# Gaps of 64 and 192 bytes between SBUF tiles, so that the operands of a transformer block's MLP lie at other remainders of 256 bytes

## The chip, the core and the metric

The kernel runs on one core of one Trainium2 chip. A time is the device time of one execution in microseconds; the median of several runs is given. One execution is also recorded by the hardware profiler, and all rows of the profile are from that one.

## The reference

One block of a diffusion transformer (PixArt style) on 16 images of 256 tokens with 256 channels, 16 heads of 16 channels, all in fp32: self-attention, cross-attention to 256 context tokens, and an MLP. Cut to what is computed:

```python
shift_a, scale_a, gate_a, shift_m, scale_m, gate_m = split(silu(c) @ W_mod + b_mod, 6)
q, k, v = heads(modulate(ln(x), shift_a, scale_a) @ W_qkv + b_qkv)
x = x + gate_a * (softmax(q @ k.T * scale) @ v @ W_proj + b_proj)
q = heads(ln(x) @ W_qc + b_qc);  k, v = heads(ln(context) @ W_kvc + b_kvc)
x = x + softmax(q @ k.T * scale) @ v @ W_cproj + b_cproj
h = gelu(modulate(ln(x), shift_m, scale_m) @ W_mlp1 + b_mlp1)      # 256 -> 1024
x = x + gate_m * (h @ W_mlp2 + b_mlp2)                             # 1024 -> 256
```

## The kernel before

**Precision.** Products of activations and weights are made of three: each operand is split into a rounded part and a rest (`...h` and `...l`, tiles of type fp32r), and `mm3` (line 411) and `mm3_tok` (line 420) add up high by high, high by low, low by high. A call of `PE.matmul` takes its stationary operand first in the source's `a` and its moving operand in `b`: 128 stationary columns, 256 moving elements.

**Attention, from the start to about 550 us.** 32 units, 16 of self- and 16 of cross-attention, are worked off in turn, each in 8 beats (`beat`, line 1041). A beat issues scores of the next unit (`s_tile`, line 661, into PSUM tile `s`, for the row maxima), transposed scores of the present one (`t_part`, line 707, into `st`, for the exponential), and beside them projections of later units (`lanes`, line 448) and the products with v (`av_part`, line 737, into `o`). Unit n keeps q and k in the SBUF tile `big[n % 3]`, so both operands of its scores are in one tile. `to_stack` (line 459) makes q and k: its `high` writes `h_...` (tag `qkh`), its `low` `l_...` (tag `qkl`), and DMAs on SP's queue carry both into `big`. `one_rows` (line 939) puts rows of ones from the tile `ones` into `big` by DMA.

**The MLP, the last 180 us.** Images go in the order 0, 2 to 15, 1; each has 4 chunks c of 256 hidden channels. For a chunk,

- `mlp_first` (line 829) multiplies with `W1`: 2 x 6 matmuls into `ph`, stationary `W1` (in `wself`), moving the transposed input `xTh_m`, `xTl_m` (tags `xTh`, `xTl`);
- `mlp_gelu` (line 860) makes `hf` (tag `pt`), `hh` (tag `qkh`) and `hl` (tag `qkl`) on ACT and POOL;
- `mlp_second` (line 877) multiplies with `W2`: 2 x 6 matmuls into `s` or `st` by turns of images, stationary `hh` and `hl`, moving `W2`, which is in `big[2]`. With the last chunk DVE makes the output (`mt`, `y`) from the gate `gm` and `xg` (`xmg` in the profile), and SP's queue stores it.

The chunks of image 1 are prepared ahead (`mlp_ahead`, line 848), and their `hh` and `hl` lie in `big[0]`. The loop at line 1239 issues for its chunk i: the gelu of i + 1, at each image's chunk 0 the transposition `mlp_T` of the next image (`psT_m`), `mlp_first` of i + 2, `mlp_second` of i - 1. Without a transposition between them, `ph` and `s`/`st` pieces of 12 matmuls alternate on TensorE. In the last four chunks there is no `mlp_first` left. `mlp_residual` (line 794) loads `gm` on SP's queue, behind the store of the image before.

**Where tiles lie.** SBUF tiles are placed one after the other in the order of their first declaration, `const` tiles (lines 78 to 143) ahead of `work` tiles, whose tags come in the order of first use with `bufs` buffers each; a size is rounded up to 32 bytes in each partition. With the sizes in bytes of a partition, the remainder of the start by 256 is:

| tiles | bytes each | start | remainder |
|---|---|---|---|
| `ident` | 512 | 17024 | 128 |
| `big0`, `big1`, `big2` | 16384 | 17568 and on | 160 |
| `v0` to `v2`, `wself`, `ones` | 4096, 16384, 1024 | 66720 and on | 160 |
| `brow`, weights of cross-attention `wqc` to `wcp` | 512, 2048 | 96416 and on | 160 |
| small tiles, `cb` (1024) at 115008 | | 113312 and on | |
| tag `qkh` (first use `c_sb`) | 3 x 2048 | 117088 | 96 |
| tag `pt` | 5 x 4096 | 123232 | 96 |
| tags `x`, `g`, `x1`, `c`, `xn` | 2048 | 143712 and on | 96 |
| tags `xTh`, `xTl` | 4 x 2048 each | 181088 | 96 |
| tag `qkl` | 3 x 2048 | 197472 | 96 |
| tag `mx`, then the rest | | 203616 and on | 96, then 224 |

The last tile ends 32 bytes below 229376. Rows, k blocks and column blocks of 128 elements inside the tiles above are multiples of 512 bytes, so an operand of an MLP matmul has its tile's remainder.

**Order.** TensorE, ACT, DVE, POOL and SP issue in program order (`InOrder`, line 40), which is written out by hand in the tables of `E_` (line 55).

Of the kernel before, what the change touches and what calls it, by code (L numbers as in the profile page):

```python
# [10 lines left out]
F32 = mybir.dt.float32  # L11
F32R = mybir.dt.float32r
# [4 lines left out]
P = 128  # L17
# [4 lines left out]
def pixart_block(  # L22
# [8 lines left out]
    B, N, H = x.shape  # L31
# [28 lines left out]
    const = ctx.enter_context(tc.tile_pool(name="const", bufs=1))  # L60
    work = ctx.enter_context(tc.tile_pool(name="work", bufs=2))
# [6 lines left out]
    def ps_gen(name, tag=None):  # L68


        if tag is None and ps_turn[0] is not None:
            ps_turn[0] ^= 1
            tag = (SHORT, LONG)[ps_turn[0]]
        tag = tag or SHORT
        return psum.tile([P, 512], F32, tag=tag, name=name, bufs=2)
# [6 lines left out]
    mhalf = const.tile([P, 2], F32, name="mhalf")  # L82
    POOL.memset(mhalf, -0.5)

    big = [const.tile([P, 2, 8, N], F32R, name=f"big{i}") for i in range(3)]
    vts = [const.tile([P, NT, NH, 32], F32, name=f"v{i}") for i in range(3)]
    wself = const.tile([P, 16, H], F32R, name="wself")
    ones = const.tile([8, N], F32, name="ones")
    DVE.memset(ones, 1.0)


    BMOD, BQKV, BQC, BKVC, BM1 = 0, 12, 18, 20, 24
    ct_ = work.tile([B, 2, H], F32, tag="qkh", name="c_sb", bufs=3)
    c_sb, th = ct_[:, 0], ct_[:, 1]
    SP.dma_start(c_sb, cond)
    X = {}
# [43 lines left out]
    bT = const.tile([P, 32], F32, name="bT")  # L140
    bP = const.tile([P, 2, 2, KC], F32, name="bP")
    sT = const.tile([P, KC, B], F32, name="sT")
    cb = const.tile([P, H], F32, name="cb")
    gd = dram.tile([B, 4, H], F32, name="gd", bufs=1)
    cd = dram.tile([1, H], F32, name="cd", bufs=1)

# [264 lines left out]
    def mm3(dst, W, f, xT):  # L411

        n = 0
        for k in range(KC):
            for a, b in ((W[0], xT[0]), (W[0], xT[1]), (W[1], xT[0])):
                PE.matmul(dst, a[:, k, f * P:(f + 1) * P], b[:, k],
                          start=(n == 0), stop=(n == 3 * KC - 1))
                n += 1
# [40 lines left out]
    def to_stack(W, src, bias, dst, which, name):  # L459

        o = Box()
        lo_row = (2, 1)[which]

        o.W, o.src, o.tok, o.name = W, src, False, name

        def first():
            o.ps = ps_gen(f"ps_{name}", LONG)
            mm3(o.ps[:, 0:N], W, 0, src.xT)  # L470

        def third():
            mm3(o.ps[:, N:], W, 1, src.xT)

        def second():
            third()
            high()

        def high():
            o.hi = work.tile([P, KC, N], F32R, tag="qkh", name=f"h_{name}", bufs=3)  # L480
            for f in range(KC):
                ACT.activation(o.hi[:, f], o.ps[:, f * N:(f + 1) * N], AF.Identity, bias=bias[f])

        def low():
            o.lo = work.tile([P, KC, N], F32R, tag="qkl", name=f"l_{name}", bufs=3)
            for f in range(KC):
                DVE.scalar_tensor_tensor(o.lo[:, f], o.ps[:, f * N:(f + 1) * N], bias[f], o.hi[:, f],
                                         ALU.add, ALU.subtract)

        def low_pool():  # L490
            o.lo = work.tile([P, KC, N], F32R, tag="qkl", name=f"l_{name}", bufs=3)
            y = work.tile([P, KC, N], F32, tag="y", name=f"y_{name}", bufs=1)
            for f in range(KC):
                ACT.activation(y[:, f], o.ps[:, f * N:(f + 1) * N], AF.Identity, bias=bias[f])
            POOL.tensor_tensor(o.lo, y, o.hi, ALU.subtract)

        def send(part, q=SP):

            row = (0, 3 - lo_row, lo_row)[part]
            q.dma_start(dst[row:row + 4 * 31 + 1:4].bitcast(F32), (o.hi if part < 2 else o.lo).bitcast(F32))  # L500

        o.send = send
        o.parts = [first, second, low]
        o.third = third
        o.low_pool = low_pool
        o.high, o.low = high, low
        o.send_high = lambda: [send(part) for part in range(2)]
        o.send_low = lambda: send(2)
        o.steps = [first, second]
        return o  # L510
# [799 lines left out]
```

## Time and profile before

| | us |
|---|---|
| median of 3 runs | 733.66 |
| lowest and highest | 732.69, 734.03 |
| the profiled execution | 732.58 |
| its span, first to last instruction | 730.8 |

The busy time of an engine is the union of its instructions. "PE" rows are matmuls, "PEld" rows loads of a stationary operand. A matmul row's own duration (0.28 us) is longer than the distance to the next one, since matmuls overlap; so distances between starts, or the length of a piece of the chain divided by its matmuls, tell the pace. A piece of the chain of waits in order of time has its start, its length in us, what ran, and the number of instructions merged in it (x12). In rows of the time line stand the start, the length, engine, line, operation, out<-in, shapes and count. All instructions have line 51, a helper's, so pieces are told apart by their tiles.

### The profile page before, as it was taken

The page shows a single profiled execution, that of the slowest core. Times are in us where ns is not written, and L with a number is a line of the kernel's source. Part 1 is how long each engine was busy: PE and PEld are TensorE (multiplying, and loading weights), DVE is VectorE, ACT ScalarE, POOL GpSimd, SP SyncE. Part 2 cuts the span into 40 slices and gives each one's busy share as a digit, 9 for nine tenths or more (in the row PEclk, how much of TensorE's full clock was granted, in tenths as well). Part 3 has the DMA queues.
Part 4 walks back from the last instruction along what each step waited for, and adds up shares of the span by engine and source line. Part 5 has one row for each costly group of instructions (what it writes and reads, how often), then busy time and mean ns, then how long its engine had stood idle before and what let it go on. Part 6 is the DMA issues. An engine that isn't in the chain of part 4 may idle for free.

```text
span 730.8 us, 22489 instructions
## 1 busy us (share of the span) xinstructions
PE 720.2 (99%) x9007; PEld 598.9 (82%) x9007; DVE 557.8 (76%) x876; ACT 557.7 (76%) x971; POOL 542.0 (74%) x533
## 2 busy tenths in 40 slices
PE   9999999999999999999999999999999999999997
PEld 8777777777777777777777778787679999999997
DVE  4878888888888788888888887878665677777743
ACT  5577888888888888888888888887867677666661
POOL 8455788887876868786686899988867988656551
PEclk9999999999999999999999999999999999999999
DMA  8365445544545555454655646456223231312212
GB/s 261 136 227 162 159 157 183 173 161 164 184 135 178 178 183 175 164 174 136 197 167 173 212 170 190 147 199 191 87 75 110 60 88 57 87 45 88 60 43 73
DMA packets 81387, 106.14 MB, mean 145 GB/s; under 512 B 16450, under 2 KB 44388, under 8 KB 81284
## 3 DMA queue, kind: packets, MB, share of 16 engines
q1 hardware_dynamic: 80180, 103.92, 44.1%
q8 instruction: 71, 1.16, 0.7%
q10 hardware_dynamic: 1104, 0.79, 0.3%
q14 instruction: 32, 0.26, 0.1%
HBM read 35.89 MB, written 8.98 MB: 61 GB/s over the span
## 4 chain that ended last, share of the span: by engine, by line
PE 93%; DVE 2%; DMA 1%; ACT 1%; POOL 1%; issue 1%; SPq 0%; ACTq 0%; POOLq 0%
PE s L51 18%; PE o L51 16%; PE st L51 14%; PE ph L51 12%; PE ps_P_s L51 4%; PE ps_k L51 4%; PE ps_qc L51 3%; PE ps_q L51 3%; PE ps_v_c L51 3%; PE ps_P_c L51 2%; PE ps_kc L51 2%; PE ps_v_s L51 2%; PE psT_c L51 2%; PE psT_s L51 1%; DVE mx L51 1%; PE psT_q L51 1%
## 5 line engine op out<-in xcount | busy, mean ns | idle before, releaser
L51 DVE TENSOR_REDUCE mx<-s 128x4 f32<-128x1024 f32 x252 | 308.1, 1222 | 88.5 <-PE s L51 85.1
L51 ACT ACTIVATE pt<-st 128x1024 f32<-128x1024 f32 x256 | 263.1, 1028 | 53.4 <-PE st L51 53.2
L51 PE MATMUL o<-pt,v 128*32 128x256 f32 x2048 | 137.0, 385 | 0.0
L51 PE MATMUL s<-big 63*128 63x256 f32 x1008 | 118.4, 307 | 1.7 <-DVE mx L51 0.7
L51 PE MATMUL st<-big 64*128 64x256 f32 (+1 forms) x1040 | 108.9, 283 | 1.6 <-DMA big<-l_q 0.8
L51 PE MATMUL ph<-xTh_m,wself 128*128 128x256 f32 x512 | 101.4, 283 | 0.0
L51 POOL TENSOR_TENSOR hl<-hf,hh 128x512 fp32r<-128x512 f32 x60 | 81.2, 1370 | 21.5 <-ACT hh L51 21.4
L51 PEld LDWEIGHTS s<-big 63*128 63x128 f32 x1008 | 78.2, 185 | 21.2 <-issue 9.3
L51 PEld LDWEIGHTS st<-big 64*128 64x128 f32 (+1 forms) x1040 | 81.9, 186 | 4.8 <-ACT pt L51 2.1
L51 PEld LDWEIGHTS o<-pt,v 128*32 128x32 f32 x2048 | 53.4, 109 | 38.9
L51 PEld LDWEIGHTS ph<-xTh_m,wself 128*128 128x128 f32 x512 | 82.7, 189 | 1.2 <-issue 0.4
L51 PE MATMUL ph<-xTl_m,wself 128*128 128x256 f32 x256 | 71.5, 279 | 0.0
L51 ACT ACTIVATE hf<-ph,bT 128x256 f32<-128x256 f32 x112 | 47.0, 473 | 21.7 <-PE ph L51 21.1
L51 ACT ACTIVATE hh<-ph,bT 128x256 fp32r<-128x256 f32 x112 | 47.2, 476 | 21.1 <-PE st L51 8.9
L51 PEld LDWEIGHTS ph<-xTl_m,wself 128*128 128x128 f32 x256 | 48.2, 188 | 0.0
L51 PE MATMUL s<-big,hh 128*128 128x256 f32 x256 | 46.0, 278 | 0.0
L51 DVE TENSOR_SCALAR xn_m<-x,mv_m,rs_m 128x256 f32<-128x256 f32 x28 | 33.6, 1239 | 14.8 <-POOL rs_m L51 14.8
L51 POOL TENSOR_SCALAR xn_c<-c,mv_c,rs_c 128x256 f32<-128x256 f32 x32 | 39.0, 1229 | 1.7
L51 PE MATMUL st<-big,hh 128*128 128x256 f32 x224 | 40.2, 278 | 0.0
L51 POOL TENSOR_SCALAR xn_q<-x,mv_q,rs_q 128x256 f32<-128x256 f32 x31 | 37.8, 1230 | 1.7
L51 PEld LDWEIGHTS s<-big,hh 128*128 128x128 f32 x256 | 39.0, 188 | 0.0
L51 ACT COPY oT<-o 128x512 f32<-128x512 f32 x64 | 37.6, 587 | 1.4 <-PE o L51 1.4
(226 smaller groups left out, 2120.9 us busy)
## 6 DMA issues: line engine op xcount, KB each, us to landing
big<-h_kc SPq DMA_DIRECT2D x32, 256.0 KB
big<-h_qc SPq DMA_DIRECT2D x32, 256.0 KB
big<-h_k SPq DMA_DIRECT2D x31, 256.0 KB
big<-h_q SPq DMA_DIRECT2D x31, 256.0 KB
big<-l_k SPq DMA_DIRECT2D x16, 256.0 KB
big<-l_q SPq DMA_DIRECT2D x16, 256.0 KB
g<-gd SPq DMA_DIRECT2D x16, 256.0 KB
U_s<-oT SPq DMA_DIRECT2D x32, 128.0 KB
```

Source lines behind the costliest of these rows:

```text
L51: i = f(*a, **k)
```

## The change

A helper `gap` declares a tile that nothing reads or writes. Six gaps are put between tiles: 192 bytes ahead of `big2` and 64 behind it, 64 ahead of the tag `qkh` and 192 behind it, 64 ahead of the tag `qkl` and 192 behind it. So `big2` (with `W2`) starts at remainder 96, and `hh` and `hl` at 160; all tiles behind each pair of gaps have the remainder that they had. To make room, `ones` no longer has a tile of its own: it is the first 8 partitions of `cb`, which is declared in its place and gets its own values later (`mlp_w1`, line 898, by a DMA on SP's queue).

```diff
-    big = [const.tile([P, 2, 8, N], F32R, name=f"big{i}") for i in range(3)]
+    def gap(pool, n, name):
+
+        pool.tile([P, n // 4], F32, tag=name, name=name, bufs=1)
+
+    big = []
+    for i in range(3):
+        if i == 2:
+            gap(const, 192, "gap_w2")
+        big.append(const.tile([P, 2, 8, N], F32R, name=f"big{i}"))
+    gap(const, 64, "gap_v")
     vts = [const.tile([P, NT, NH, 32], F32, name=f"v{i}") for i in range(3)]
     wself = const.tile([P, 16, H], F32R, name="wself")
-    ones = const.tile([8, N], F32, name="ones")
+    cb = const.tile([P, H], F32, name="cb")
+    ones = cb[:8]
     DVE.memset(ones, 1.0)
...
+    gap(work, 64, "gap_h")
     ct_ = work.tile([B, 2, H], F32, tag="qkh", name="c_sb", bufs=3)
+    gap(work, 192, "gap_pt")
...
-    cb = const.tile([P, H], F32, name="cb")
...
         def low():
+            if name == "k0":
+                gap(work, 64, "gap_l")
             o.lo = work.tile([P, KC, N], F32R, tag="qkl", name=f"l_{name}", bufs=3)
+            if name == "k0":
+                gap(work, 192, "gap_mx")
```

## The prediction, on record before the result

> **What bounds the kernel now.** I read the page first: how busy each engine is, the granted clock, and what the chain that ended last is made of.
>
> ```profile
> span 730.8 us, 22489 instructions
> PE 720.2 (99%) x9007; PEld 598.9 (82%) x9007; DVE 557.8 (76%) x876; ACT 557.7 (76%) x971; POOL 542.0 (74%) x533
> ...
> PEclk9999999999999999999999999999999999999999
> ...
> PE 93%; DVE 2%; DMA 1%; ACT 1%; POOL 1%; issue 1%; SPq 0%; ACTq 0%; POOLq 0%
> ```
>
> TensorE is busy 99% of the span at full granted clock and makes up 93% of the chain. Only a change in the spacing of its matmuls can move the end by much. So the second view is the chain in order of time, in the stage where the MLP runs alone (from about 549 us). A piece is a run of matmuls into one PSUM tile: `ph` is a chunk of the first MLP product, `s` or `st` a chunk of the second, each of 12 matmuls of one form (128 rows, 128 columns, 256 moving elements). One image, which begins with its transposition (`psT_m`):
>
> ```profile
> 594.22 0.44 PE psT_m L51 x4
> 594.66 1.39 PE ph L51 x12
> 596.05 1.36 PE st L51 x12
> 597.41 1.42 PE ph L51 x12
> 598.83 1.41 PE s L51 x12
> 600.24 1.38 PE ph L51 x12
> 601.62 1.36 PE s L51 x12
> 602.98 1.42 PE ph L51 x12
> 604.39 1.42 PE s L51 x12
> ```
>
> Nothing stands between the pieces: TensorE waits for nobody here. Yet equal work has two lengths, 1.36 us (113 ns a matmul) and 1.42 us (118 ns), and they alternate: short `ph` and short `s`/`st`, then long `ph` and long `s`/`st`, then again. Other engines' work is no likely cause, because beside the last chunks there is almost none of it (the rows of DVE below are from there) and the spacing is longest of all. For this I looked at the time line of the end:
>
> ```profile
> 718.69 0.69 DVE L51 TENSOR_TENSOR xmg<-x,gm 128x512 f32<-128x512 f32 x1 [4.35 <-DMA gm<-gd]
> ...
> 719.93 0.76 DVE L51 TENSOR_TENSOR mt<-s,gm 128x256 f32<-128x256 f32 x2 [0.55 <-PE s L51]
> ```
> ```profile
> 719.73 5.91 PE L51 MATMUL st<-big,big 128*128 128x256 f32 x48
> ```
>
> Those 48 matmuls take 5.91 us, the last one's own 0.28 us included: (5.91 - 0.28) / 47 = 119.8 ns. They are the chunks of image 1, the only ones with both operands in `big` tiles.
>
> What else differs is where the operands lie. The time line with weight loads (PEld) shows that the next matmul's stationary operand is read beside the present one's moving operand:
>
> ```profile
> 587.32 0.28 PE L51 MATMUL st<-big,hl 128*128 128x256 f32 x1
> 587.32 0.30 PEld L51 LDWEIGHTS st<-big,hh 128*128 128x128 f32 x2
> ...
> 587.44 0.40 PE L51 MATMUL st<-big,hh 128*128 128x256 f32 x2
> ```
>
> Two loads start at 587.32 and the next matmul 0.12 us later, so load and stream share the same tenth of a microsecond. From the declarations, with sizes rounded up to 32 bytes, `big` and `wself` start at remainder 160 of 256 bytes and the large `work` tiles at 96; every row and column block inside is a multiple of 256. The offset stationary minus moving is then +64 in `ph` (weights 160, `xT` 96), -64 in `s`/`st` (`hh`, `hl` 96, `W2` 160), and 0 in image 1's chunks (both 160) and at every seam between a `ph` and an `s`/`st` piece. The slowest spacing, 119.8 ns, is where the offset is 0 throughout. And the length changes at one kind of seam: from a short `s`/`st` to a long `ph`, from a long one to a shorter one. The seam from `ph` to `s`/`st` keeps it.
>
> **The change part by part.** Its gaps add 64 and 192 bytes and no instruction. After it `big2` (which holds `W2`) is at 96, `hh` and `hl` at 160, everything else of the MLP where it was. So `s`/`st` goes from -64 to +64, image 1 from 0 to +64, all seams from 0 to +64: the MLP becomes one uniform stream, as inside a `ph` piece today.
>
> What a uniform stream does is shown before the loop, by two runs of two `ph` pieces in a row:
>
> ```profile
> 545.31 2.94 PE ph L51 x24
> 548.25 1.00 PE o L51 x16
> 549.26 3.02 PE ph L51 x24
> ```
>
> The first run is 0.08 us shorter, which is 16 of its matmuls at 113 ns in place of 118: it starts long and goes over to short. The second is 24 x 118 ns = 2.83 us and a start and an end of 0.1 us each, long throughout. So an offset of +64 keeps either spacing; it doesn't force the short one. But the first `ph` after a transposition always ends short: 1.39 us, with 0.03 us more than 1.36 for its start, and the `s`/`st` behind it is 1.36 each time. The transpositions' operands (`ident`, `xn`, then `wself`) keep their remainders, so I expect this start again, 13 times. With no seam at offset 0 behind it, the short spacing then lasts until the next transposition.
>
> The terms, from the pieces between 558 and 719.9 us, of which these are the first and last of each kind:
>
> ```profile
> 558.51 1.39 PE ph L51 x12
> 559.90 1.36 PE s L51 x12
> 561.26 1.42 PE ph L51 x12
> 562.68 1.41 PE st L51 x12
> 564.10 1.37 PE ph L51 x12
> ...
> 698.94 1.39 PE ph L51 x12
> ...
> 708.67 1.42 PE st L51 x12
> 710.09 1.38 PE ph L51 x12
> 711.46 1.36 PE st L51 x12
> 712.82 1.42 PE ph L51 x12
> 714.24 5.67 PE s L51 x48
> ```
>
> - 27 `ph` at 1.42 become 1.36: 27 x 0.06 = 1.62 us.
> - 10 `s`/`st` at 1.41 and 16 at 1.42 become 1.36: 10 x 0.05 + 16 x 0.06 = 1.46 us.
> - 6 `ph` at 1.37 and 8 at 1.38 become 1.36: 0.06 + 0.16 = 0.22 us.
> - The four chunks of 5.67 become 4 x 1.36 = 5.44: 0.23 us.
> - 13 `ph` at 1.39 and 27 `s`/`st` at 1.36 stay.
>
> Sum 3.53 us. Image 1's 48 matmuls would gain 47 x 6.5 ns = 0.3 us, but they are not on the chain. This is what is there:
>
> ```profile
> 721.91 3.67 DMA gm<-gd
> 725.58 0.02 issue
> 725.61 0.11 DVE xmg L51
> ...
> 726.22 0.76 DVE mt L51 x2
> ```
>
> The gate's DMA lands at 725.58 and TensorE ends at 719.73 + 5.91 = 725.64; `mt` starts at 726.22. The DMA follows the chunk that ended at 719.9, so it comes forward by the whole 3.5 us and the gain inside image 1 is worth nothing. Ahead of it `xmg` ends at 718.69 + 0.69 = 719.38, and `mt` waits for TensorE until 719.93: 0.55 us of cover, of which the 0.23 us above take less than half. The other engines are at 76% or less and don't become the bound for 2% of a stage.
>
> **Taking `cb` into the place of `ones`** could add a wait on SP's queue: the load of `cb` must come after the readers of `ones`.
>
> ```profile
> L51 SPq DMA_DIRECT2D big<-ones x6: 635/644/775, 10.4 to 37.8; - x6
> ```
> ```profile
> L51 SPq DMA_DIRECT2D cb<-cd x1: 422/422/422, 406.7 to 406.7; - x1
> ```
>
> The last reader is issued at 37.8 us, the load at 406.7. The distance hides it; nothing behind it on SP waits. Cost 0.
>
> **Attention** is the unknown cost. A third of the units keep q and k in `big2`. Inside such a unit both operands move together, so offset 0 stays 0, but seams to neighbours change. In about 20 of 32 units the seam from scores (`s`) to transposed scores (`st`), 8 a unit, goes from 0 to +64 or -64. The seams to the projections and back go both ways, because those have weights at 160 in one row half and at 96 in the other. The trace has no such seam in isolation. The nearest rows give 119.8 - 113.3 = 6.5 ns for offset 0 against the short spacing; 160 seams x 6.5 ns = 1.0 us, as a gain or, if the other seams lose it, as a cost. I take 0, because gains and losses of one kind stand against each other, and keep 1.0 us at both ends.
>
> So the sum is -3.5 us: 732.58 us of the profiled execution becomes 729.1. That execution lies 1.1 us below the median of the runs, 733.66, which becomes **730.2 us**.
>
> One rule speaks against it. The Trainium skill, "TensorE: Matmul & The Clock Gate", section "Step-by-step: what each phase is for", says that TensorE has two independent SBUF read ports and that loading the next weights takes no read bandwidth from the running matmul. By that rule the sum would be 0 and the time 733.66. The trace's 113 and 119.8 ns for one form do not look like it, but no run here yet has the same chunk at two offsets.
>
> **The rivals.**
> - *The offset is not the cause* (what alternates is something periodic, such as ACT's and POOL's work on the chunks). For it: the image's whole schedule is periodic too. Against it: the 119.8 ns with nearly nothing beside. Time 733.7.
> - *The seam changes the spacing because the stream moves to other tiles*, not because of offset 0. The alternation then survives in part. For it: only one of the two seams with offset 0 changes anything. About half of the 3.5 us is left: 732.0.
> - *The uniform stream stays long* (slower). If after a short `s`/`st` the transposition does not start a short `ph`, nothing later changes it back. The 3.02 us pair shows that +64 can stay long for 24 matmuls, and today a long `s`/`st` always precedes a transposition, so the other case is untested. Price: 27 `s`/`st` x 0.06 = 1.62, 14 `ph` from 1.37 or 1.38 to 1.42 = 6 x 0.05 + 8 x 0.04 = 0.62, 13 `ph` from 1.39 = 0.39; together +2.6 us, 736.3. It decides in the first five matmuls after `psT_m`, and costs more than it gains as soon as over half of the images start long.
>
> **How the numbers follow.** Forecast 0.55 (its own range 728.9 to 731.5: 1.0 us for attention and some tenths for the spread of runs), no effect 0.14, half 0.17, slower 0.14. About 0.2%, 1.5 us, is what a measurement of this kernel tells from no change. Faster: 0.55 and half of the half case, 0.63; within: 0.14 + 0.09 = 0.23; slower 0.14. The range leaves out the slow case and the outer edges: 728.8 to 734.4.
>
> **What would show it.** In the chain after: all `ph` and `s`/`st` pieces at 1.36, save one `ph` of 1.39 behind each `psT_m`; image 1's 48 matmuls near 5.6 us instead of 5.91; the same length from 0 to 540 us within 1 us. If the alternation stays, the seam's offset is not what starts it. If all pieces are 1.42, the short spacing is not reached from a short predecessor. If 48 matmuls of image 1 still take 5.91 us at +64, the offset does not matter at all. If the time is gained or lost before 540 us, the seams of attention were not small.

## The result, and the profile after

| | before | after |
|---|---|---|
| median of 20 runs each, us | 733.94 | 730.22 |
| lowest and highest | 732.31, 742.04 | 728.92, 738.14 |

The changed kernel takes 0.9953 of the time before, with a 95% interval of 0.9932 to 0.9974: it is faster, by 3.7 us, and the prediction was 730.2.

The page of the changed kernel, the lines that answer to those of before:

```profile
span 736.3 us, 22489 instructions
PE 723.5 (98%) x9007; PEld 601.5 (82%) x9007; DVE 562.5 (76%) x876; ACT 557.4 (76%) x971; POOL 541.6 (74%) x533
...
PEclk7899999999999999999999999999999999999999
```

The span is longer than that of before, 730.8 us, although the median is shorter. The first digits of the granted clock tell why: this one execution (738.14 us, the highest of the 20) was given less clock at its start. The view by stretches says how much (us of the stretch, then busy time and instructions of PE, PEld, DVE, ACT and POOL, the granted clock, the share of the DMA engines and their GB/s), first in the kernel before and then in the changed one:

```profile
0.00:36.50 36.50, 33.79 (x246) 28.75 (x247) 22.60 (x52) 20.94 (x39) 24.07 (x33) 1.00 0.59 198
```
```profile
0.00:36.80 36.80, 32.84 (x195) 30.05 (x196) 19.49 (x46) 15.52 (x31) 20.32 (x27) 0.77 0.57 188
36.80:556.00 519.20, 515.92 (x7279) 398.21 (x7277) 422.91 (x649) 427.81 (x671) 400.35 (x402) 1.00 0.51 166
```

At a mean clock of 0.77 (in stretches of 4 us it is 0.50 from 12 to 24 us), 195 matmuls fit in the first 36.8 us, where before had 246 in 36.5. From there on the clock is 1.00, so the pieces of the MLP can be read in this trace; the whole length is read in a second profile of the same kernel, `again_5` below, whose span is 728.0 us. The kernel before has such executions as well: on the chips of the experiments, 738.7 to 740.5 us at a mean clock of 0.99.

One image in the chain of waits of the changed kernel, in order of time:

```profile
602.45 0.57 PE psT_m L51 x4
603.02 1.38 PE ph L51 x12
604.39 1.36 PE st L51 x12
605.75 1.36 PE ph L51 x12
...
612.55 1.37 PE s L51 x12
613.92 0.44 PE psT_m L51 x4
```

The alternation is gone: behind the transposition comes one `ph` of 1.38 and then nothing above 1.37. All 13 images begin like that. (The image ahead of this one ends with an `st` of 1.61, which holds a wait of 0.15 us for POOL's `hl`.) And image 1 on the time line:

```profile
725.33 5.60 PE L51 MATMUL st<-big,big 128*128 128x256 f32 x48
```

(5.60 - 0.28) / 47 = 113.2 ns a matmul, where before had 119.8.

**Where the time came from.** The chain of `again_5`, the first regular piece of the MLP and the last one:

```profile
559.09 1.38 PE ph L51 x12
...
711.66 5.45 PE s L51 x48
```

From its first `ph` to the end of the four last chunks it takes 711.66 + 5.45 - 559.09 = 158.02 us; before took 714.24 + 5.67 - 558.51 = 161.40. The stage is 3.38 us shorter. It began 0.58 us later, at 559.09 and not 558.51 (about 0.3 us of that is a wait for POOL's `hl` at the entrance of the MLP). So in these two profiles the gain is in the MLP, piece by piece, and none of it ahead; 3.38 less 0.58 is the 2.8 us between the spans of 730.8 and 728.0. The medians of 20 runs lie further apart, 3.7 us.

### The profile page after: what moved, and what is told of

It reads as the page before. It is cut to its first block, busy times and chain, and to the rows that moved or that the text cites. A ratio compares the mean times of both kernels' runs of the same rounds, so it can differ in the third digit from the quotient of the medians.

```text
span 736.3 us, 22489 instructions
## 1 busy us (share of the span) xinstructions
PE 723.5 (98%) x9007; PEld 601.5 (82%) x9007; DVE 562.5 (76%) x876; ACT 557.4 (76%) x971; POOL 541.6 (74%) x533
## 4 chain that ended last, share of the span: by engine, by line
PE 93%; DVE 3%; DMA 1%; ACT 1%; issue 1%; POOL 0%; ACTq 0%; SPq 0%
PE s L51 17%; PE o L51 16%; PE st L51 15%; PE ph L51 12%; PE ps_qc L51 4%; PE ps_k L51 4%; PE ps_q L51 4%; PE ps_P_s L51 4%; PE ps_v_c L51 3%; PE ps_kc L51 3%; PE ps_v_s L51 2%; PE ps_P_c L51 2%; PE psT_c L51 2%; PE psT_s L51 2%; DVE mx L51 2%; PE psT_q L51 1%
## 5 line engine op out<-in xcount | busy, mean ns | idle before, releaser
L51 PE MATMUL ph<-xTh_m,wself 128*128 128x256 f32 x512 | 99.6, 280 | 0.0
L51 PE MATMUL ps_k<-xTh_s,wself 64*128 64x256 f32 (+1 forms) x232 | 39.0, 293 | 0.1
```

The source lines that it names most:

```text
L51: i = f(*a, **k)
```

## The experiments

The theory is that the spacing is set by the **offset**: the remainder of a stationary operand's start by 256 bytes, minus that of the moving operand beside which it is loaded. At a seam, where one piece follows another, that is the first stationary operand of the new piece beside the last moving operand of the old one. A uniform +64 keeps a short spacing of 113 ns; an offset of 0 is slow in itself and, at a seam, turns short into long. The rivals are that

- any change of tiles at a seam turns the spacing;
- any offset but 0 is good;
- each product's own offset counts and the seams do nothing;
- for what remained, the remainders of the transposition decide.

All edits are to the changed kernel. The table says where each puts the offsets (bytes; "seam 1" is from `ph` to `s`/`st`, "seam 2" back), and what came out. Long is 1.41 to 1.44 us a piece, short is 1.36 to 1.38; the few pieces between which last projections of attention (`psP_c`) run are left aside. `t_uniform` and `qk_apart`, which move other operands too, stand behind.

| kernel | `ph` | `s`/`st` | seam 1 | seam 2 | image 1 | pieces of the loop | median us |
|---|---|---|---|---|---|---|---|
| before | +64 | -64 | 0 | 0 | 0 | two short, two long | 733.94 |
| after | +64 | +64 | +64 | +64 | +64 | short | 730.22 |
| `w2_only` | +64 | 0 | 0 | +64 | +64 | long | 737.29 |
| `hidden_only` | +64 | 0 | +64 | 0 | 0 | `ph` mostly short, `s`/`st` long | 735.82 |
| `mixed` | +64 | -64 | -64 | +64 | +64 | short | 730.49 |
| `seam_fs` | +64 | +64 | 0 | 128 | 128 | `ph` long, `s`/`st` short | 733.78 |
| `seam_sf` | +64 | +64 | 128 | 0 | 0 | `ph` short, `s`/`st` long | 734.35 |
| `all_128` | 128 | 128 | 128 | 128 | +64 | long | 738.04 |
| `all_32` | +32 | +32 | +32 | +32 | +64 | long | 736.32 |
| `all_minus64` | -64 | -64 | -64 | -64 | +64 | whole images short or long | 733.10 |

Each run stands beside the kernel before on its own chip, with medians of 733.51 to 734.12 us. The ratios below are to that kernel, with their 95% intervals; they differ a little from the quotients of the medians.

### The changed kernel again

No edit; run twice, to see how steady the pieces are.

> The changed kernel once more, for a profile without the low clock of its first slices. Offset theory (stationary minus moving remainder; a stream at +64 without seams at 0 keeps the short spacing): 730.2 us, pieces of ph and s/st at 1.36 us, image 1's 48 matmuls at 113 ns. Chance theory (the short pieces of the one profile were luck, since +64 can keep either spacing): another pattern of pieces, 1.36 and 1.42 mixed, time between 730 and 734.

> The changed kernel, to stand beside the other two on the same chip: 730.2 us by the result so far, 729.5 to 731.

Measured: 731.18 us, ratio 0.9943 (0.9903 to 0.9984), and 731.02 us, ratio 0.994 (0.9912 to 0.9969). `again_5` had no long image. `again` had three of 13. The image ahead of one of them, and that one, in its chain:

```profile
663.28 0.44 PE psT_m L51 x4
...
674.63 0.44 PE psT_m L51 x4
675.06 1.42 PE ph L51 x12
676.48 1.41 PE s L51 x12
...
686.37 0.44 PE psT_m L51 x4
```

The second image starts long and stays long for all 8 pieces, until the next transposition. It takes 686.37 - 674.63 = 11.74 us, the one ahead of it 674.63 - 663.28 = 11.35: 0.4 us dearer. So +64 keeps either spacing, and the start behind `psT_m` chooses.

### Half of the change

`w2_only` drops the gaps around the tags `qkh` and `qkl`; `hidden_only` keeps those and drops the gaps around `big2`. In both, `s`/`st` comes to offset 0.

```diff
-    gap(work, 64, "gap_h")
-    gap(work, 192, "gap_pt")
...
-                gap(work, 64, "gap_l")
-                gap(work, 192, "gap_mx")
```

> Only the gaps around big2: W2 at 96, hh and hl back at 96. Offsets: ph +64, s/st 0, image 1 +64; seam ph to s/st 0, s/st to ph +64. Offset theory: s/st pieces at 120 ns, 1.44 us; ph pieces long or short. About 56 s/st pieces on the chain by 0.08 us more than in the changed kernel is 4.5 us, with all ph long another 3: 734.7 to 738 us; image 1 at 113 ns. If only seams matter and not the offset within a piece: one kind of seam at 0 is left, 730 to 734, no piece over 1.42. If offsets don't matter: 733.9.

```diff
-            gap(const, 192, "gap_w2")
-    gap(const, 64, "gap_v")
```

> Only the gaps around hh and hl: both at 160, W2 back at 160. Offsets: ph +64, s/st 0, image 1 0; seam ph to s/st +64, s/st to ph 0. Offset theory: s/st at 1.44 us, 734.7 to 738 us; image 1 at 119.8 ns. So each half of the change by itself loses, and only both together gain. If offsets within a piece don't matter: 730 to 734, no piece over 1.42.

Measured: `w2_only` 737.29 us, ratio 1.0064 (1.0037 to 1.0092); `hidden_only` 735.82 us, ratio 1.0027 (1.0017 to 1.0038). Each half alone is slower than no change. The chain of `w2_only`:

```profile
655.64 1.42 PE ph L51 x12
657.05 1.44 PE s L51 x12
```

The same 12 matmuls of `W2` take 1.44 us at offset 0 (120 ns), 1.41 or 1.42 at -64 before when long, and 1.36 when short. The chain of `hidden_only`:

```profile
656.49 1.44 PE s L51 x12
657.93 1.37 PE ph L51 x12
659.31 1.42 PE st L51 x12
```

`ph`, whose own operands never moved, is long throughout in the one kernel and mostly short in the other: it depends on what runs ahead of it. The four kernels together show that neither operand of `s`/`st` sets the pace alone: with `hh` and `W2` at 96 and 96 or at 160 and 160 the pieces are long, with 160 and 96 short, with 96 and 160, as before, some of each. One miss: image 1 has +64 in `w2_only`, and yet its time line shows

```profile
724.33 5.82 PE L51 MATMUL st<-big,big 128*128 128x256 f32 x48
```

which is (5.82 - 0.28) / 47 = 117.9 ns. It follows long pieces and stays long for 48 matmuls. In `hidden_only`, at 0, the same row has 5.92 us, 120.0 ns.

### Other tiles, or other offsets, at the seam

`mixed` puts `hh` and `hl` at 32: the seams go to other tiles and to offsets of other sign, but none is 0.

```diff
-    gap(work, 64, "gap_h")
+    gap(work, 192, "gap_h")
-    gap(work, 192, "gap_pt")
+    gap(work, 64, "gap_pt")
...
-                gap(work, 64, "gap_l")
+                gap(work, 192, "gap_l")
-                gap(work, 192, "gap_mx")
+                gap(work, 64, "gap_mx")
```

> hh and hl at 32, W2 at 96: ph at +64 as before the change, s/st at -64 as before the change, but the seams at -64 (ph to s/st) and +64 (s/st to ph) in place of 0. Offset theory: no seam at 0, so the short spacing lasts: 730.2 us, all pieces 1.36. Rival (the spacing changes wherever a stream goes over to other tiles or another offset): the alternation of 1.36 and 1.42 stays, 733.9. Rival (only +64 can be short): s/st at 1.42, about 733.5.

Measured: 730.49 us, ratio 0.9959 (0.9944 to 0.9973), and all pieces short save two beside `psP_c`:

```profile
662.25 0.44 PE psT_m L51 x4
662.69 1.38 PE ph L51 x12
664.07 1.36 PE st L51 x12
665.43 1.36 PE ph L51 x12
```

The tiles change at each seam and the sign of the offset at both, and nothing flips. So the rival that other tiles or another offset turn the spacing falls.

### One seam at 0

`seam_fs` and `seam_sf` keep +64 inside all products and put one seam at 0; the other is then at 128.

```diff
-            gap(const, 192, "gap_w2")
+            gap(const, 128, "gap_w2")
-    gap(const, 64, "gap_v")
+    gap(const, 128, "gap_v")
-    gap(work, 64, "gap_h")
-    gap(work, 192, "gap_pt")
...
-                gap(work, 64, "gap_l")
-                gap(work, 192, "gap_mx")
```

> W2 at 32, hh and hl at 96: ph and s/st both at +64, but the seam from ph to s/st is at 0 and that from s/st to ph at 128. In the kernel before, this seam kept the spacing. Offset theory as the traces so far refine it: all pieces short, 1.36 us, save those of an image that starts long; 730.2 us. If any seam at 0 changes the spacing: 1.36 and 1.42 alternate, 733.9.

`seam_sf` has no gaps around `big2`, and the four gaps of the work tiles are 128:

> W2 at 160, hh and hl at 224: ph and s/st both at +64, the seam from s/st to ph at 0 and that from ph to s/st at 128. In the kernel before, this seam changed the spacing each time. Offset theory: short and long pairs alternate as in the kernel before, ph and s/st 1.36 and then 1.42, 733.7 us. Rival (no seam matters, only a uniform offset in the pieces): 730.2 us.

Measured: `seam_fs` 733.78 us, ratio 0.9984 (0.9957 to 1.0012), a miss; `seam_sf` 734.35 us, ratio 1.0003 (0.9977 to 1.003), the time about as expected, but not the pattern: pieces alternate one by one, where pairs had been expected. One image in the chain of `seam_fs`, from its start:

```profile
618.55 0.44 PE psT_m L51 x4
618.98 1.38 PE ph L51 x12
620.36 1.42 PE st L51 x12
621.78 1.42 PE ph L51 x12
623.19 1.38 PE s L51 x12
624.57 1.41 PE ph L51 x12
```

A short `ph`, across seam 1 (0) a long `st`; across seam 2 (128) a `ph` that is long too; across seam 1 an `s` of 1.38, which goes over to short (0.02 us more than 1.36 is some four matmuls at 118 in place of 113 ns); across seam 2 a long `ph` again. In `seam_sf`, where the offsets of the seams are exchanged:

```profile
630.81 0.44 PE psT_m L51 x4
631.25 1.39 PE ph L51 x12
632.64 1.41 PE s L51 x12
634.05 1.38 PE ph L51 x12
```

So a seam at 128 leaves a long piece behind it, whatever comes ahead; a seam at 0 turned short into long and long into short. So the rival that the seams do nothing falls, since all products of the loop have +64 of their own in both kernels. That seam 1 "keeps" the spacing, as it seems in the trace of before, does not hold here: in `seam_fs` it turns it.

### The whole MLP at 128, at 32, at -64

A gap ahead of `wself` moves `W1` as well, so that all offsets of the loop are one value. The three kernels differ in sizes only; this is `all_128`:

```diff
+    gap(const, 64, "gap_ws")
     wself = const.tile([P, 16, H], F32R, name="wself")
+    gap(const, 192, "gap_cb")
...
-    gap(work, 64, "gap_h")
+    gap(work, 128, "gap_h")
-    gap(work, 192, "gap_pt")
+    gap(work, 128, "gap_pt")
...
-                gap(work, 64, "gap_l")
+                gap(work, 128, "gap_l")
-                gap(work, 192, "gap_mx")
+                gap(work, 128, "gap_mx")
```

> All of the MLP but image 1 at +128 (moving at 96, stationary at 224), seams too; the projections of self-attention go to 128 as well. Offset theory (whatever is not 0 does): 730.2 us, pieces at 1.36. If the distance repeats at 128 bytes, 128 acts as 0: pieces at 1.44, about 738 to 739 us.

> All of the MLP but image 1 at +32 (moving at 96, stationary at 128), seams too; the projections of self-attention go to 32 as well. If 32 bytes are apart enough: 730.2 us, pieces at 1.36 or, for images that start long, 1.42. If what collides is 64 bytes wide or the two reads drift by that much, 32 acts as 0: pieces at 1.44, 738 to 739 us.

> All of the MLP but image 1 at -64 (moving at 96, stationary at 32), seams too; the projections of self-attention with q and k go to -64 and those with v to +64. If only the distance of 64 bytes counts and not its sign: 730.2 to 731 us, pieces at 1.36 save those of single images that start long. If the stationary operand must be ahead: pieces at 1.42 throughout, about 736.

Measured: `all_128` 738.04 us, ratio 1.0061 (1.0023 to 1.0099); `all_32` 736.32 us, ratio 1.0026 (1.0009 to 1.0043); `all_minus64` 733.10 us, ratio 0.9987 (0.9969 to 1.0004). `all_128` took the time that the rival of 128 acting as 0 had given; `all_32` and `all_minus64` lie between the two times expected of each. A uniform stream at 128 or at 32 is long from end to end. The chain of `all_128`, and that of `all_32`:

```profile
665.98 1.43 PE ph L51 x12
667.40 1.42 PE st L51 x12
```
```profile
658.43 1.42 PE ph L51 x12
659.85 1.43 PE st L51 x12
```

1.42 to 1.43 us are 118 to 119 ns. Image 1 kept +64 in both, and behind such pieces it is short. The time line of `all_32`:

```profile
723.90 5.60 PE L51 MATMUL st<-big,big 128*128 128x256 f32 x48
```

So "any offset but 0" falls: of 0, 32, 64 and 128 only 64 has the short spacing. At -64 whole images are one or the other. Two images of `all_minus64`:

```profile
612.82 0.44 PE psT_m L51 x4
613.25 1.37 PE ph L51 x12
...
624.14 0.44 PE psT_m L51 x4
624.58 1.42 PE ph L51 x12
```

6 of its 13 images are short and 7 long. The sign doesn't matter for keeping a spacing, but +64 starts nearly always short (13 of 13, 10 of 13 and 13 of 13 in the three profiles of the changed kernel) and -64 about half of the time in its one profile.

### What starts an image

The transposition (`ident`, `xn`) runs ahead of each image. `t_uniform` moves `ident` behind `big2`, to 96, and `xn` to 160, so that its seams are no longer as they were.

```diff
-    ident = const.tile([P, P], F32, name="ident")
-    make_identity(nc, ident)
...
+    ident = const.tile([P, P], F32, name="ident")
+    make_identity(nc, ident)
     gap(const, 64, "gap_v")
...
+            if name == "s0":
+                gap(work, 64, "gap_xn")
...
+            if name == "s0":
+                gap(work, 192, "gap_xt")
```

> The changed kernel with the transpositions at +64 too (ident at 96, xn at 160), so that the seams from s/st to psT (0 before), inside psT (-32) and from psT to ph (+32) are all at +64. If the seam of the transposition decides whether an image starts short: all images start short, no long one as at 674.8 us of the repeated run; up to 0.4 us less than the changed kernel, 729.8 to 730.2. If the start depends on something else (when the transposition's input comes): images that start long still appear in some runs, 730.2 to 731.

Measured: 731.17 us, ratio 0.9984 (0.9955 to 1.0012), not to be told from the changed kernel's own 731.02 on the same chip; the interval takes in 1, so by itself this run doesn't show a gain over before either. Three of its 13 images start long, as in `again`; one of them in the chain:

```profile
627.90 0.44 PE psT_m L51 x4
628.34 1.42 PE ph L51 x12
```

So these remainders alone do not decide the start. It is no toss of a coin either: in `t_uniform` the long images are the third, seventh and eleventh, and in `all_minus64` every second one from the sixth on. What makes this pattern stays open.

### Scores of attention at 64

In attention q and k of a unit lie in one tile, so their scores have offset 0. `qk_apart` splits each `big` into two tiles with 64 bytes between them, and moves `hl` to 224, so that in the MLP, too, the stationary operand loaded beside each moving one is 64 bytes further on.

```diff
-            gap(const, 192, "gap_w2")
-        big.append(const.tile([P, 2, 8, N], F32R, name=f"big{i}"))
-    gap(const, 64, "gap_v")
+            gap(const, 64, "gap_w2")
+        bq = const.tile([P, 8, N], F32R, name=f"bigq{i}")
+        gap(const, 64, f"gap_k{i}")
+        big.append((bq, const.tile([P, 8, N], F32R, name=f"bigk{i}")))
...
-                gap(work, 64, "gap_l")
+                gap(work, 128, "gap_l")
-                gap(work, 192, "gap_mx")
+                gap(work, 128, "gap_mx")
```

> The changed kernel, and in attention k 64 bytes further on than q: q and k in tiles of their own (remainders 160 and 224, 224 and 32, 96 and 160), so that scores and transposed scores run at +64 or -64 in place of 0; of the seams from s to st two of three kinds leave 0 and one goes to 128. W2's low half then lies at 160, and hl goes to 224, so that every moving operand still stands beside a stationary one 64 bytes further on. Offset theory: 4 matmuls of s and 4 of st in each of 256 beats, in pairs; 2 or 3 of the distances a beat fall from 117-121 ns to 113-118: 1.5 to 4 us less than the changed kernel, 726 to 729 us, gained between 0 and 550 us; the MLP unchanged with pieces of 1.36. If the offset acts only in matmuls of all 128 rows: 730.2, as the changed kernel.

Measured: 734.51 us, ratio 1.0014 (0.9994 to 1.0033). Both parts missed. The groups of scores (busy us, mean ns of one, idle before), first of `again_5`, where q and k are at offset 0, then of `qk_apart`:

```profile
L51 PE MATMUL s<-big 63*128 63x256 f32 x1008 | 118.2, 307 | 1.3 <-DVE mx L51 0.7
L51 PE MATMUL st<-big 64*128 64x256 f32 x1024 | 107.0, 283 | 0.8 <-ACT pt L51 0.8
```
```profile
L51 PE MATMUL s<-bigk,bigq 63*128 63x256 f32 x1008 | 117.3, 306 | 2.1 <-DVE mx L51 0.7 <-DMA U_s<-oT 0.4 <-DVE st_q L51 0.4
L51 PE MATMUL st<-bigq,bigk 64*128 64x256 f32 x1024 | 106.3, 282 | 0.7 <-ACT pt L51 0.7
```

Matmuls of 63 and 64 rows hardly react: 118.2 to 117.3 and 107.0 to 106.3 us, under 1%, and none of it reaches the MLP, whose first `ph` starts at 560.28 us, 1.2 us later than in `again_5`. In the MLP of `qk_apart`, from its chain:

```profile
561.66 1.41 PE s L51 x12
563.07 1.38 PE ph L51 x12
```

`s`/`st` is always long, although the load beside each stream has +64 everywhere. What differs from the changed kernel is that the moving operands now change between 96 and 160 from one matmul to the next, and that two of the three products have other offsets of their own: `hh` with the low half of `W2` is at 0 (both at 160), `hl` with the high half at 128. Either could be the cause; no run separates them. That the operand loaded beside a stream counts, and not only a product's own, is therefore shown at the seams alone.

## Why the prediction was right

- **The bound and the place.** TensorE's spacing in the MLP was read as the only thing that can move the end, and all of the gain is there: 3.38 us of the stage against a sum of 3.53. The difference is of the size of the rounding: most images end with an `s`/`st` of 1.37, not 1.36, and the last four chunks take 5.45, not 5.44. That the median met the forecast to 0.02 us is luck: the same kernel had 731.18 and 731.02 us in the two repeats, 2.6 and 2.7 us below the kernel before beside them.
- **The pieces.** 27 long `ph`, 26 long `s`/`st` and 14 partly long `ph` went to 1.36 to 1.38 in the changed kernel and in `again_5`, save two or three pieces beside the last projections of attention (`psP_c`), which run between them, and the one `st` that waited for `hl`. That the offset is the cause, and not something periodic beside it, is shown by `w2_only` and `hidden_only`: the same program order, with `s`/`st` at offset 0, is slower than before. The lengths of their pieces carry the times, too: in `w2_only` the 27 shorter `ph` of before grow to 1.42 (6 x 0.05 + 8 x 0.04 + 13 x 0.03 = 1.01 us) and the `s`/`st` to 1.44 (27 x 0.08 + 16 x 0.02 + 10 x 0.03 = 2.78); with the 733.75 of before on the same chip that makes 737.5, and 737.29 was measured.
- **The Trainium skill's rule** ("TensorE: Matmul & The Clock Gate", section "Step-by-step: what each phase is for"), by which a weight load takes no read bandwidth from the running matmul, would have left the time at 733.66. The runs disagree: one form of matmul takes 113, 118 or 120 ns by nothing but the place of its operands. The measurement decides. What slows the matmuls inside the chip, the runs do not show.
- **The uniform stream holds its spacing**: shown in both directions, by short images of the changed kernel and by the long ones in `again` and `all_minus64`. So the slower rival had a real mechanism. What kept it from deciding is that the start behind `psT_m` was short in 36 of 39 images. That was expected for a reason that did not hold: the transposition's operands keep their remainders, yet `W2`, which is read just ahead of it, moved, so that the seam into the transposition went from -64 to 0; and `t_uniform`, which moved them all, starts much the same. With no known cause for the short start, the forecast was in this part lucky. In `all_minus64`, where half start long, the time can't be told from before.
- **Two statements were too broad.** That offset 0 is what is slow: 32 and 128 are long as well, and only 64, of either sign, was seen short. And that the seam from `ph` to `s`/`st` keeps the spacing: true of the trace of before, but in `seam_fs` the same seam at the same offset turns it. Neither touched the sum, since the change leaves no seam between `ph` and `s`/`st` at 0.
- **Seams of attention at 0** (with 1.0 us either way): right. The stage began within 0.6 us of before, and `qk_apart` shows that even all scores at 64 in place of 0 save less than 1% of their busy time.
- **`cb` in the place of `ones`, and image 1**: right. `w2_only` and `hidden_only` have `cb` there too and are slower than before, so the gain is not from it. Image 1's 48 matmuls went from 5.91 to 5.60 us, and the chain behind them still goes through the gate's DMA:

```profile
727.51 3.61 DMA gm<-gd
```

- **A reading of the loads.** The row of two loads at 587.32 us is merged: each takes 0.19 us and the row 0.30, so the second starts 0.11 us behind the first. That a load runs beside the present matmul stands all the same.
- **No version beat the changed kernel.** `mixed` (730.49) and `t_uniform` (731.17) lie within its own spread.

## What to carry to other kernels

Where TensorE alone bounds a stage of back-to-back matmuls and equal pieces of its chain differ by some per cent, work out where the operands start: in this kernel all moving operands at one remainder of 256 bytes and all stationary ones 64 bytes further on was the fast layout, and `mixed`, with -64 in one product and at one seam, was as fast. Move both sides or neither, because half of the move was slower than none. And judge by the lengths of the pieces: here the start behind one transposition set the pace of the 96 matmuls behind it.

## What the runs showed of the hardware that was not expected

- The spacing of this matmul (128 rows, 128 columns, 256 moving elements) has two stable values at offsets of +64 and -64, 113.2 ns and 117.9 ns, and keeps the one it has for at least 96 matmuls, a whole image. At 0 it is 120 ns, at 32 and 128 between 118 and 119.
- A seam with offset 128 left long pieces behind it in both kernels that had one between such products. A seam at 0 turned the spacing in `seam_fs`, in `seam_sf` and at one of the two in before, not at the other. Seams at +64 and -64 turned nothing between products at +64 and -64.
- What chooses the spacing behind a transposition is open: not the remainders of `ident` and `xn` (`t_uniform`), and in runs of one and the same kernel 0, 0 and 3 of 13 images started long. Why the place of an operand counts is open, too. The remainder by 256 orders these runs and that by 128 would not, since seams at 0 and at 128 act differently; no run tests a longer period.
- The granted clock was 0.50 from 12 to 24 us in one execution of the changed kernel (0.77 in the mean of the first 37 us), and 1.00 there in another, `again_5`, of the same program. The profiles of `all_128` and `all_minus64` show the same fall, with a mean of 0.81.
